# Selective-scan layers on one core: two scan tiles per step instead of one, and one activation table set for exp and ln

## The chip, the cores and the metric

The kernel runs on one core of a Trainium2 chip. The metric is device microseconds of one execution. The engines are named as in the profile: PE is TensorE's matmul (PEld its weight loads), DVE is VectorE, ACT is ScalarE, POOL is GpSimd, SP is SyncE, whose queue issues the DMAs.

## The reference

A stack of four layers acts on four images of 64 x 64 tokens with 96 channels. Every layer is a normalisation, a mixer with a residual, another normalisation and a feed-forward block in a small float format with a residual. Layer 0's mixer is a gated recurrence over the 4096 tokens with 16 states per channel. The mixers of layers 1 to 3 project to 192 channels, convolve 3 x 3, and run a selective scan in four directions; cut to what matters, it is

```python
delta = softplus(dts + bias)
def step(h, inp):
    u_l, dl, b_l, c_l = inp
    dA = jnp.exp(dl[..., None] * A)
    h = dA * h + (dl * u_l)[..., None] * b_l[:, :, None, :]
    y = jnp.einsum('bkdn,bkn->bkd', h, c_l)
    return (h, y)
_, ys = lax.scan(step, h0, (u_t, d_t, B_t, C_t))
y = ys + Dp * u
```

The four directions are added, normalised, multiplied by silu(z) and projected back to 96 channels.

## The kernel before, in words

The kernel writes the order of each engine's instructions out by hand: a wrapper (class `InOrder`, line 71) chains all instructions of one engine in the order in which the program emits them. Since this wrapper makes every instruction, all rows of the profile carry its line, L78, and are told apart by the names of their tiles.

There are three stretches. `gated` (line 1034) does layer 0 for all images: 32 strips of 512 tokens with 12 tiles each. `scans` (line 839) does layers 1 to 3, which are 12 stages (an image and a layer), and a tail does what is left of the last image.

A stage of `scans` has 24 items: two directions of time, four segments of 1024 tokens, three chunks of 128 channel rows (a row is a channel in one of two orders of the tokens). An item has 16 tiles, one for each state n, so there are 12 x 24 x 16 = 4608 tiles. For one tile [128, 1024]

- `c_rows` (line 867) reads the C row of state n from DRAM, broadcast over 64 partitions, by two DMAs into a `c` buffer (six of them);
- `decays` (line 877) makes `da` = exp(delta * A) on ACT (three buffers);
- `b_rows` (line 883) broadcasts the B row into PSUM by two matmuls of `sel` with `bs`, tile `bc`; there are two such buffers, so the B rows of one tile wait until the scan two tiles before has read its own;
- `scan` (line 892) multiplies `bc` by `du` = delta * u on DVE, in place ("product" below), and then runs the recurrence over the 1024 tokens as one TENSOR_TENSOR_SCAN into `h` (three buffers);
- `carry` (line 908) copies the last state out on ACT, `times_c` (line 914) multiplies `h` by `c` on POOL;
- `accumulate` (line 934) adds the result over the states in PSUM (`acc`, one buffer) by eight matmuls of 64 x 64 (sixteen at an item's first tile); `take` (line 945) copies the sum out on ACT, and `store` (line 949) writes it by four DMAs.

The loop at line 975 takes one tile k per step: carry k-1, C rows and decays k+2, B rows k+1, times_c k-1, product k, `beside`, scan k, accumulate k-3. `beside` (line 999) puts side work between product and scan: it pumps the chains that prepare the next item (`prepare_chunk`, line 805: matmuls, softplus, du) and the next segment (line 775), and takes a step of a job. A job (line 717) is everything else: the mixers' ends, feed-forward, input projections and convolutions of the stage before or after, cut into pieces at each `yield`; `rate` pieces of every chain run per tile.

ScalarE evaluates exp, ln, softplus, silu and sigmoid from tables, and a load is put in front of an activation whose function isn't in the set that is loaded. A norm is `measure` (line 217: mean and variance), a logarithm, and `settle` (line 232: exp(-0.5 ln v), refined on POOL). The norms queue in `pending`, and `logarithms` (line 242) does all that are queued together: behind a softplus, at n = 11 of each item, or when a job had no other work for `patience` pumps. Chains wait until their norm is `known`.

Of the kernel before, what the change touches and what calls it, by code (L numbers as in the profile page):

```python
# [13 lines left out]
F8 = mybir.dt.float8e5  # L14
# [85 lines left out]
def metaformer(ctx: ExitStack, tc: tile.TileContext, x, l0_ab, l0_rest, ssm, ffn, out):  # L100
# [31 lines left out]
    def settle():  # L132
        banks["free"] += banks["back"]
        banks["back"] = 0

    def pump(chain):

        if chain is None or chain.done:
            return False
        if callable(chain.need):  # L140
            if not chain.need():
                return False
        elif chain.need and banks["free"] < 1:
# [13 lines left out]


    ident = const("ident", [128, 128])
    make_identity(nc, ident)  # L160
# [7 lines left out]

    mod32 = sb(3, "h", [NB3, 32])
    dve.tensor_tensor(mod32, ident[0:NB3, 0:32], ident[0:NB3, 32:64], ALU.add)  # L170
# [12 lines left out]
    dve.tensor_tensor(fold, fold, ident[:, 96:128], ALU.add)  # L183
    ones = const("ones", [128, 1])
    pool.memset(ones, 1.0)
    minus = const("minus", [128, 1])
    pool.memset(minus, -1.0)
    small = {}
# [6 lines left out]
    for layer in range(4):  # L195
        raw = sb(3, "da", [128, F_N])
        sp.dma_start(out=raw, in_=ffn[layer])
        w1 = const(f"w1_{layer}", [C, HID], F8)
        dve.tensor_copy(w1, raw[0:C, 0:HID], saturate=False)
        w2 = const(f"w2_{layer}", [128, 3, C], F8)  # L200
        dve.tensor_copy(w2, raw[:, F_W2:F_B1].rearrange("p (h c) -> p h c", h=3), saturate=False)
        b8 = sb(3, "h", [128, 3 + C], F8)
        dve.tensor_copy(b8, raw[:, F_B1:F_N], saturate=False)
        b = const(f"b_{layer}", [128, 3 + C])
        dve.tensor_copy(b, b8)
        ffw.append((w1, w2, b))


    class Norm:


        def __init__(self):
            t = sb(13, "norm", [128, 3, G])
            self.v, self.r, self.nm = (t[:, i, :] for i in range(3))
            self.known = False

        def measure(self, src, width, e):
# [11 lines left out]
            act.activation(self.nm, mv[:, :, 0], AF.Copy, scale=-1.0)  # L229
            pending.append(self)  # L230

# [6 lines left out]


    pending = []  # L240

    def logarithms():
        for n in pending:
            act.activation(n.r, n.v, AF.Ln)
            n.known = True
        pending.clear()

# [322 lines left out]
    def convolve(im, layer, s, hold):  # L570
# [20 lines left out]
        for i, v in enumerate(raw):  # L591
            act.activation(v, v, AF.Silu, bias=w[:, W_CB + i : W_CB + i + 1])
        gate_z(im, s + 1, hold)
        yield
        yield
# [27 lines left out]
    def between(im, layer, dst=None):  # L623
# [32 lines left out]
        def mixers():  # L656
            for s in range(NSTRIP):
                yield lambda: done["end"] > s - 2 and (
                    layer == 0 or (done["y"] > s and hold["y", s][1].known)
                )  # L660
                if layer:
# [5 lines left out]
        def feeds():  # L667
            for s in range(NSTRIP):
                yield lambda: done["x"] > s and hold["x", s][1].known
                yield from feed_forward(im, layer, s, hold, new)  # L670
                done["end"] += 1
# [31 lines left out]
        def convolves():  # L703
            yield lambda: done["in"] > 0
            gate_z(im, 0, hold)
            yield
            yield
# [9 lines left out]
    class Job:  # L717


        def __init__(self, rounds, rate=1.4, patience=17):  # L720
            self.rounds, self.rate, self.credit = rounds, rate, 0.0
            self.patience, self.waited = patience, 0
            self.chains, self.done = [], False

        def step(self):
            self.credit = min(self.credit + self.rate, 3.0)
            while self.credit >= 1 and not self.done:
                self.credit -= 1
                while not self.done and all(c.done for c in self.chains):
                    if pending:  # L730
                        break
# [4 lines left out]
                if any([pump(c) for c in self.chains]) or not pending:  # L736
                    self.waited = 0
                    continue
                self.waited += 1
                if self.waited >= self.patience:  # L740
                    logarithms()
                    self.waited = 0

        def finish(self, eager=False):

            while not self.done:
                self.step()
                if eager and pending:
                    logarithms()
                settle()  # L750
# [54 lines left out]
    def prepare_chunk(item):  # L805
# [16 lines left out]
        act.activation(delta, delta, AF.Softplus)  # L822
        logarithms()
        yield
# [14 lines left out]
    def scans(stages, jobs, pac):  # L839
# [51 lines left out]

        def scan(k, beside):
            i, n = tiles[k]
            da, b = live.pop((k, "da")), live.pop((k, "b"))
            dve.tensor_tensor(b, i.du, b, ALU.mult)
            beside()
            h = live[k, "h"] = sb(3, "h", [128, T])
            step = slice(None, None, -1 if i.d else 1)
# [15 lines left out]
        def times_c(k):  # L914
            i, n = tiles[k]
            c = live[k, "c"]
            pool.tensor_tensor(c, live.pop((k, "h")), c, ALU.mult)

# [41 lines left out]
        start(items[0])  # L960
        c_rows(0)
        c_rows(1)
        decays(0)
        decays(1)
        b_rows(0)
        working = []
# [7 lines left out]

        for k in range(last + 5):
            q, n = divmod(k, NS)
            if k <= last:
                item = items[q]
                nxt = at(q + 1)
                if n == 0:  # L980
                    if q % per == 0:
# [4 lines left out]
                    chain = Chain(prepare_chunk(nxt), True) if nxt is not None else None  # L986
                if item.chunk == 1 and n == 4 and at(q + 2) is not None:
                    if q % per == per - 2:
# [4 lines left out]
                    segment = Chain(next_segment(items[q + 2 : q + 5]))  # L993
                if n == 8 and nxt is not None:
                    start(nxt)
                if n == 8 and nxt is not None and nxt.d == 1:
                    nxt.yf = sb(2, "y", [128, T])
                    sp.dma_start(out=nxt.yf, in_=nxt.im.y[nxt.chunk, :, nxt.seg * T : (nxt.seg + 1) * T])
            def beside():
# [8 lines left out]
            full = items[(k - 4) // NS] if k >= 4 and (k - 4) % NS == NS - 1 else None  # L1008
            if full is not None:
                take(full)  # L1010
            if 0 <= k - 1 <= last:
                carry(k - 1)
            if k + 2 <= last:
                c_rows(k + 2)
                decays(k + 2)
            if n == 11:
                logarithms()
            if k + 1 <= last:
                b_rows(k + 1)
            if 0 <= k - 1 <= last:  # L1020
                times_c(k - 1)
            if k <= last:
                scan(k, beside)
            if full is not None:
                store(full)
            if 0 <= k - 3 <= last:
                accumulate(k - 3)
            settle()
        while working:
# [4 lines left out]
    def gated(images, job, pac):  # L1034
# [6 lines left out]
        rest = sb(1, "e", [128, T])  # L1041
        sp.dma_start(out=rest[0:C, 0:L0_BIAS], in_=l0_rest[0:C, 0:L0_BIAS])
# [22 lines left out]
        def prepare(st):  # L1065
# [3 lines left out]
            yield  # L1069
            logarithms()  # L1070
            yield
            yield from norm.settle()
# [6 lines left out]
            pool.tensor_scalar(var, var, 1e-3, None, ALU.add)  # L1079
            pending.append(again)  # L1080
            yield
            logarithms()
            yield
            act.activation(again.r, again.r, AF.Exp, scale=-0.5)
# [21 lines left out]
            yield  # L1106
            act.activation(st.gate, ps[0:C], AF.Sigmoid, bias=col(at)[0:C])
            release()
            pair = [sb(2, t, [128, T]) for t in ("delta", "du", "y")]
# [68 lines left out]
        def recur(t):  # L1178
# [5 lines left out]
            dve.scalar_tensor_tensor(db, db, col(LT + i), st.du[g], ALU.add, ALU.mult)  # L1184
            h = t["h"] = sb(3, "h", [128, T])[:, 0:MM]
            dve.tensor_tensor_scan(
# [86 lines left out]
    with tc.tile_pool(name="pbig", bufs=2, space=bass.MemoryType.PSUM) as wides_pool:  # L1273
        wides.append(wides_pool)
        with tc.tile_pool(name="pl0", bufs=1, space=bass.MemoryType.PSUM) as pl0:
            gated(images, Job(between(images[0], 0), 2.6, patience=1), pl0)
        stages = [(im, layer) for layer in range(1, 4) for im in images]
# [12 lines left out]
    with tc.tile_pool(name="pend", bufs=6, space=bass.MemoryType.PSUM) as pend:  # L1290
        banks.update(free=6, back=0, pool=pend)
        Job(between(images[-1], 3, images[-1].dst), 3, patience=1).finish(eager=True)

# [115 lines left out]
```

## Time and profile before

| | us |
|---|---|
| median of 3 runs | 19251.46 (19226.88 to 19251.56) |
| the profiled execution | 19244.18 |
| its span, first to last instruction | 19242.4 |
| mean granted TensorE clock | 0.800 |

A row of groups in the profile has line, engine, operation, out<-in, shapes, count; then busy us and the mean duration of one in ns; then the engine's idle time just before these instructions and what ended most of it. A row in order of time has start and length in us, the engine, the operation, and in brackets an idle time of the engine before it. Two rows of one engine can overlap, where the next instruction starts before the end of the one before it.

The granted clock in tenths over the span, in 40 slices, and the matmul engine's busy tenths:

```profile
PE   8998787787787788788888788788888788788887
...
PEclk9998796786787797797797797797787787788775
```

The table loads are a group of their own:

```profile
L78 ACT ACT_TABLE_LOAD x1287 | 1651.2, 1283 | 37.7 <-DVE mv L78 19.8
```

### The profile page before, as it was taken

The numbers are of one execution on the slowest core, as the hardware profiler recorded it, in microseconds if no ns is written. First come the engines' busy times: TensorE is split into PE (matmuls) and PEld (weight loads), VectorE is DVE, ScalarE is ACT, GpSimd is POOL, SyncE is SP. The second block draws the span as 40 slices with busy tenths as digits, with TensorE's granted clock in tenths as the row PEclk, the third lists the DMA queues.
The fourth block names the chain that finished last, engine by engine and source line by source line (L and its number), as shares of the span: only waits on it lengthen the run. The fifth ranks groups of instructions, "written<-read, shape, count | busy, mean of one in ns | idle before, by whom it ended". The sixth has DMA issues, their size and how long they took to land.

```text
span 19242.4 us, 219783 instructions
## 1 busy us (share of the span) xinstructions
PE 15910.7 (83%) x69248; PEld 4675.9 (24%) x69248; DVE 17682.6 (92%) x13768; ACT 11062.2 (57%) x17831; POOL 13533.8 (70%) x9222
## 2 busy tenths in 40 slices
PE   8998787787787788788888788788888788788887
PEld 3332121121122222222222222222222222222323
DVE  6757999999999999999999999999999999999985
ACT  4544564555555665665665665665665665666664
POOL 3434777777777777777777777777777777777775
PEclk9998796786787797797797797797787787788775
DMA  2213666666676667667667677667676676676664
GB/s 52 51 45 93 167 189 170 167 187 171 167 194 176 171 186 185 172 186 183 171 187 182 174 191 182 170 187 187 168 192 180 171 192 179 170 198 176 168 180 115
DMA packets 1269846, 3192.04 MB, mean 166 GB/s; under 512 B 440336, under 2 KB 440560, under 8 KB 1262544
## 3 DMA queue, kind: packets, MB, share of 16 engines
q1 hardware_dynamic: 1268688, 3177.97, 62.7%
q8 instruction: 559, 9.16, 0.2%
q14 instruction: 599, 4.91, 0.1%
HBM read 2818.51 MB, written 308.28 MB: 162 GB/s over the span
## 4 chain that ended last, share of the span: by engine, by line
DVE 62%; PE 17%; ACT 10%; issue 4%; DMA 3%; POOL 3%; SPq 1%; DVEq 1%; POOLq 0%; ACTq 0%
DVE h L78 43%; DVE bc L78 16%; ACT da L78 5%; PE bc L78 4%; PE acc L78 4%; PE conv L78 2%; ACT L78 2%; DMA c<-cs 2%; POOL c L78 1%; PE dt_proj L78 1%; SPq L78 1%; DVE st L78 1%; PE y_t L78 1%; PE c L78 1%; POOL du L78 1%
## 5 line engine op out<-in xcount | busy, mean ns | idle before, releaser
L78 POOL TENSOR_TENSOR c<-h,c 128x1024 f32<-128x1024 f32 (+1 forms) x4992 | 11337.3, 2274 | 5052.2 <-DVE h L78 3027.9
L78 DVE TENSOR_TENSOR_SCAN h<-da,carry,bc 128x1024 f32<-128x1024 f32 x4608 | 10798.8, 2343 | 559.6 <-POOL c L78 53.5
L78 PE MATMUL acc<-c,twice 64*64 64x512 f32 x36864 | 6386.0, 770 | 35.5 <-POOL c L78 31.2
L78 ACT ACTIVATE da<-delta,decay 128x1024 f32<-128x1024 f32 x4608 | 5285.0, 1148 | 1687.0 <-DVE h L78 1680.0
L78 PE MATMUL bc<-bs,sel 96*128 96x512 bf16 x9216 | 3509.2, 470 | 2769.7 <-DVE h L78 2671.1
L78 DVE TENSOR_TENSOR bc<-du,bc 128x1024 f32<-128x1024 f32 x4608 | 5567.0, 1208 | 181.5 <-PE bc L78 170.8
L78 ACT COPY carry<-h 128x1 f32<-128x1 f32 x3456 | 652.8, 189 | 3929.1 <-DVE h L78 3924.3
L78 PEld LDWEIGHTS <-sel 96*128 96x128 bf16 x9216 | 563.8, 102 | 7896.7 <-DVE h L78 6245.7
L78 PEld LDWEIGHTS acc<-c,twice 64*64 64x64 f32 x36864 | 1149.8, 156 | 2898.8 <-issue 2020.8
L78 ACT ACT_TABLE_LOAD x1287 | 1651.2, 1283 | 37.7 <-DVE mv L78 19.8
L78 PE MATMUL conv<-pad,tap_lo 128*128 128x512 f32 x1728 | 918.7, 638 | 0.0
L78 PE MATMUL dt_proj<-rows,w 12*128 12x512 f32 x1152 | 841.3, 817 | 6.4 <-ACT delta L78 3.9
L78 ACT COPY y<-acc 128x1024 f32<-128x1024 f32 x288 | 291.6, 1012 | 808.6 <-PE acc L78 785.8
L78 PE MATMUL x_proj<-u,xp 128*108 128x512 f32 x1152 | 715.0, 739 | 20.2 <-DMA xp<-in_ssm 8.5
L78 POOL TENSOR_TENSOR du<-delta,u 128x1024 f32<-128x1024 f32 x288 | 678.9, 2357 | 1.5 <-issue 1.5
L78 ACT ACTIVATE c<-c,l_bias 128x512 f32<-128x512 f32 x384 | 263.4, 686 | 658.4 <-PE c L78 655.7
L78 PE MATMUL conv<-pad,tap_hi 128*128 128x512 f32 (+1 forms) x1152 | 606.8, 630 | 1.6 <-ACT u L78 1.6
L78 DVE TENSOR_TENSOR_SCAN h<-da,l_carry,bc 128x512 f32<-128x512 f32 x384 | 491.5, 1280 | 42.4 <-DVE bc L78 1.8
L78 PE MATMUL y_t<-ident,pad 128*128 128x128 f32 (+1 forms) x1536 | 389.2, 340 | 51.3 <-DMA pad<-y 40.6
L78 PE MATMUL bc<-rows,u 96*128 96x512 f32 x768 | 395.4, 640 | 41.6 <-DVE h L78 41.6
L78 PEld LDWEIGHTS conv<-pad,tap_lo 128*128 128x128 f32 x1728 | 339.7, 204 | 324.4 <-issue 255.1
L78 PE MATMUL bc<-xp,u 96*128 96x512 f32 x768 | 391.0, 634 | 24.2 <-DVE h L78 24.0
(143 smaller groups left out, 12353.1 us busy)
## 6 DMA issues: line engine op xcount, KB each, us to landing
c<-cs SPq DMA_DIRECT2D x9216, 256.0 KB, 4.2
u<-u SPq DMA_DIRECT2D x288, 512.0 KB, 6.7
y<-y SPq DMA_DIRECT2D x1152, 128.0 KB, 3.5
y<-y SPq DMA_DIRECT2D x144, 512.0 KB, 6.2
xr<-x SPq DMA_DIRECT2D x224, 192.0 KB, 5.0
u<-u SPq DMA_DIRECT2D x288, 128.0 KB, 3.9
pad<-y SPq DMA_DIRECT2D x288, 128.0 KB, 4.8
z<-zl SPq DMA_DIRECT2D x96, 256.0 KB, 4.5
```

The source lines that it names most:

```text
L78: ins = f(*a, **k).ins
```

## The change

The loop over tiles takes two tiles a and b = a + 1 per step. Product and scan are separate functions, and a step emits: decays b; carry a-2 and b-2; decays a+2; times_c b-2; for a-4 and then b-4: accumulate and the C rows of the tile six later; product a; `beside`; product b; scan a; `beside`; B rows a+2; times_c a; scan b; B rows b+2; and in the second step of an item `take` and `store` of the item before. There are four `h` buffers instead of three. The queue of norms, `known` and `patience` are gone: each norm's logarithm is emitted with its measuring, and `exp_and_ln` loads a table set that holds both exp and ln behind every softplus, sigmoid and group of silus. Layer 0's small weights share a buffer with its last block of weights. The diff, cut to its core:

```diff
+    def exp_and_ln():
+
+        act.preload_act_table_set("natural_log_exp_and_others")
...
             act.activation(self.v, mv[:, :, 1], AF.Identity, bias=small[e])
             act.activation(self.nm, mv[:, :, 0], AF.Copy, scale=-1.0)
-            pending.append(self)
+            act.activation(self.r, self.v, AF.Ln)
...
-                yield lambda: done["x"] > s and hold["x", s][1].known
+                yield lambda: done["x"] > s
...
         act.activation(delta, delta, AF.Softplus)
-        logarithms()
+        exp_and_ln()
...
-        def scan(k, beside):
+        def times_b(k):
+            i, n = tiles[k]
+            b = live[k, "b"]
+            dve.tensor_tensor(b, i.du, b, ALU.mult)
+
+        def scan(k):
             i, n = tiles[k]
             da, b = live.pop((k, "da")), live.pop((k, "b"))
-            dve.tensor_tensor(b, i.du, b, ALU.mult)
-            beside()
-            h = live[k, "h"] = sb(3, "h", [128, T])
+            h = live[k, "h"] = sb(4, "h", [128, T])
...
+            if on:
+                decays(b)
+            for k in (a - 2, b - 2):
+                if 0 <= k <= last:
+                    carry(k)
+            if a + 2 <= last:
+                decays(a + 2)
+            if 0 <= b - 2 <= last:
+                times_c(b - 2)
+                del live[a - 2, "h"], live[b - 2, "h"]
+            for k in (a - 4, b - 4):
+                if 0 <= k <= last:
+                    accumulate(k)
+                if k + 6 <= last:
+                    c_rows(k + 6)
+            if on:
+                times_b(a)
+            beside(2 * m)
+            if on:
+                times_b(b)
+                scan(a)
+            beside(2 * m + 1)
+            if a + 2 <= last:
+                b_rows(a + 2)
+            if on:
+                times_c(a)
+                scan(b)
+            if b + 2 <= last:
+                b_rows(b + 2)
+            if m == 1 and q >= 1:
+                take(items[q - 1])
+                store(items[q - 1])
...
             act.activation(st.gate, ps[0:C], AF.Sigmoid, bias=col(at)[0:C])
+            exp_and_ln()
```

More of the change, by code (lines that the diff above doesn't have):

```diff
@@ L166, in metaformer @@
     stacked = twice[:, 0:64]
-    mod32 = sb(3, "h", [NB3, 32])
+    mod32 = sb(4, "h", [NB3, 32])
     dve.tensor_tensor(mod32, ident[0:NB3, 0:32], ident[0:NB3, 32:64], ALU.add)
@@ L183, in metaformer @@
     dve.tensor_tensor(fold, fold, ident[:, 96:128], ALU.add)
[L184 to L187, printed above, removed]
     small = {}
@@ L201, in metaformer @@
         dve.tensor_copy(w2, raw[:, F_W2:F_B1].rearrange("p (h c) -> p h c", h=3), saturate=False)
-        b8 = sb(3, "h", [128, 3 + C], F8)
+        b8 = sb(4, "h", [128, 3 + C], F8)
         dve.tensor_copy(b8, raw[:, F_B1:F_N], saturate=False)
@@ L214, in __init__ @@
             self.v, self.r, self.nm = (t[:, i, :] for i in range(3))
-            self.known = False
         def measure(self, src, width, e):
@@ L237, in settle @@
             pool.tensor_tensor(self.nm, self.nm, self.r, ALU.mult)
[L240 to L246, printed above, removed]
     def refine(r, v):
@@ L657, in mixers @@
             for s in range(NSTRIP):
-                yield lambda: done["end"] > s - 2 and (
-                    layer == 0 or (done["y"] > s and hold["y", s][1].known)
-                )
+                yield lambda: done["end"] > s - 2 and (layer == 0 or done["y"] > s)
                 if layer:
@@ L705, in convolves @@
             gate_z(im, 0, hold)
+            exp_and_ln()
             yield
@@ L717, in metaformer, with __init__ @@
     class Job:
-        def __init__(self, rounds, rate=1.4, patience=17):
+        def __init__(self, rounds, rate=1.4):
             self.rounds, self.rate, self.credit = rounds, rate, 0.0
-            self.patience, self.waited = patience, 0
             self.chains, self.done = [], False
@@ L729, in step @@
                 while not self.done and all(c.done for c in self.chains):
-                    if pending:
-                        break
                     self.chains = next(self.rounds, None)
@@ L735, in step, with finish @@
                     break
[L736 to L740, printed above, removed]
-                    logarithms()
-                    self.waited = 0
-        def finish(self, eager=False):
+                for c in self.chains:
+                    pump(c)
+        def finish(self):
             while not self.done:
                 self.step()
-                if eager and pending:
-                    logarithms()
                 settle()
@@ L822, in prepare_chunk @@
         act.activation(delta, delta, AF.Softplus)
-        logarithms()
+        exp_and_ln()
         yield
@@ L916, in times_c @@
             c = live[k, "c"]
-            pool.tensor_tensor(c, live.pop((k, "h")), c, ALU.mult)
+            pool.tensor_tensor(c, live[k, "h"], c, ALU.mult)
         def add_quarters(i, v, lhs, start, stop):
@@ L960, in scans @@
         start(items[0])
-        c_rows(0)
-        c_rows(1)
+        for k in range(2):
+            c_rows(k)
+            b_rows(k)
         decays(0)
-        decays(1)
-        b_rows(0)
         working = []
@@ L973, in work @@
                 working[0].step()
-        for k in range(last + 5):
-            q, n = divmod(k, NS)
-            if k <= last:
+        half = NS // 2
+        for j in range(len(tiles) // 2 + 2):
+            q, m = divmod(j, half)
+            a, b = 2 * j, 2 * j + 1
+            on = b <= last
+            if on:
                 item = items[q]
                 nxt = at(q + 1)
-                if n == 0:
+                if m == 0:
                     if q % per == 0:
@@ L986, in scans @@
                     chain = Chain(prepare_chunk(nxt), True) if nxt is not None else None
-                if item.chunk == 1 and n == 4 and at(q + 2) is not None:
+                if item.chunk == 1 and m == 2 and at(q + 2) is not None:
                     if q % per == per - 2:
@@ L993, in scans, with beside @@
                     segment = Chain(next_segment(items[q + 2 : q + 5]))
-                if n == 8 and nxt is not None:
+                if m == 4 and nxt is not None:
                     start(nxt)
[L996 to L999, printed above, removed]
+                    if nxt.d == 1:
+                        nxt.yf = sb(2, "y", [128, T])
+                        t = slice(nxt.seg * T, (nxt.seg + 1) * T)
+                        sp.dma_start(out=nxt.yf, in_=nxt.im.y[nxt.chunk, :, t])
+            def beside(n):
                 pump(chain)
@@ L1006, in beside @@
                 work()
[L1008 to L1028, printed above, removed]
+                settle()
+            if on:
[22 more added lines that the diff above has]
+                b_rows(a + 2)
+            if on:
+                times_c(a)
[5 more added lines that the diff above has]
+                store(items[q - 1])
         while working:
@@ L1040, in gated @@
             sp.dma_start(out=v[0:C, 0:n], in_=l0_ab[:, i * T : i * T + n])
-        rest = sb(1, "e", [128, T])
+        rest = blocks[-1][:, 3 * LT * 128 - 4 * T : T]
         sp.dma_start(out=rest[0:C, 0:L0_BIAS], in_=l0_rest[0:C, 0:L0_BIAS])
@@ L1069, in prepare @@
             yield
-            logarithms()
-            yield
             yield from norm.settle()
@@ L1079, in prepare @@
             pool.tensor_scalar(var, var, 1e-3, None, ALU.add)
-            pending.append(again)
             yield
-            logarithms()
-            yield
+            act.activation(again.r, var, AF.Ln)
             act.activation(again.r, again.r, AF.Exp, scale=-0.5)
@@ L1107, in prepare @@
             act.activation(st.gate, ps[0:C], AF.Sigmoid, bias=col(at)[0:C])
+            exp_and_ln()
             release()
@@ L1184, in recur @@
             dve.scalar_tensor_tensor(db, db, col(LT + i), st.du[g], ALU.add, ALU.mult)
-            h = t["h"] = sb(3, "h", [128, T])[:, 0:MM]
+            h = t["h"] = sb(4, "h", [128, T])[:, 0:MM]
             dve.tensor_tensor_scan(
@@ L1275, in metaformer @@
         with tc.tile_pool(name="pl0", bufs=1, space=bass.MemoryType.PSUM) as pl0:
-            gated(images, Job(between(images[0], 0), 2.6, patience=1), pl0)
+            gated(images, Job(between(images[0], 0), 2.6), pl0)
         stages = [(im, layer) for layer in range(1, 4) for im in images]
@@ L1291, in metaformer @@
         banks.update(free=6, back=0, pool=pend)
-        Job(between(images[-1], 3, images[-1].dst), 3, patience=1).finish(eager=True)
+        Job(between(images[-1], 3, images[-1].dst), 3).finish()
 def _layer0(W_in, b_in, W_out, b_out, gamma, beta):
```

## The prediction

> **What bounds the kernel now.** I read the page's busy shares first, then the groups of instructions, then VectorE in order of time, then who waits for whom, last the stretches of one stage.
>
> ```profile
> PE 15910.7 (83%) x69248; PEld 4675.9 (24%) x69248; DVE 17682.6 (92%) x13768; ACT 11062.2 (57%) x17831; POOL 13533.8 (70%) x9222
> ...
> L78 DVE TENSOR_TENSOR_SCAN h<-da,carry,bc 128x1024 f32<-128x1024 f32 x4608 | 10798.8, 2343 | 559.6 <-POOL c L78 53.5
> ...
> L78 DVE TENSOR_TENSOR bc<-du,bc 128x1024 f32<-128x1024 f32 x4608 | 5567.0, 1208 | 181.5 <-PE bc L78 170.8
> L78 PE MATMUL bc<-bs,sel 96*128 96x512 bf16 x9216 | 3509.2, 470 | 2769.7 <-DVE h L78 2671.1
> ```
>
> VectorE is busy 92%; the 4608 scans and 4608 products are 16.4 of its 17.7 ms. The scans' idle time is 559.6 us, yet its largest named releaser explains only 53.5. VectorE in order of time shows the rest:
>
> ```profile
> 9002.12 1.23 DVE L78 TENSOR_TENSOR bc<-du,bc 128x1024 f32<-128x1024 f32 x1
> 9003.48 2.35 DVE L78 TENSOR_TENSOR_SCAN h<-da,carry,bc 128x1024 f32<-128x1024 f32 x1
> ...
> 9010.60 1.21 DVE L78 TENSOR_TENSOR bc<-du,bc 128x1024 f32<-128x1024 f32 x1
> 9011.72 0.41 DVE L78 BATCH_NORM_STATS2 st<-x 128x6 f32<-128x96 f32 x2
> 9012.04 2.33 DVE L78 TENSOR_TENSOR_SCAN h<-da,carry,bc 128x1024 f32<-128x1024 f32 x1
> 9014.29 1.21 DVE L78 TENSOR_TENSOR bc<-du,bc 128x1024 f32<-128x1024 f32 x1
> ```
>
> A scan right behind its product starts 0.13 us after the product's end (9002.12 + 1.23 = 9003.35, start 9003.48). An instruction that doesn't read its forerunner starts 0.09 us before that one's end (9010.60 + 1.21 = 9011.81, start 9011.72; 9012.04 + 2.33 = 9014.37, start 9014.29). So a dependent pair costs 0.13 + 0.09 = 0.22 us. A tile then takes 1.12 + 0.22 + 2.26 = 3.60 us, and in the trace's records 3143 of 4607 scan-to-scan distances are 3.59 to 3.61. From the first scan (1775) to the last one's end (19027) VectorE is the bound; ahead of it lies the gated layer, where PE is busy 1571 of 1775 us, behind it a tail of 216 us.
>
> PE is the engine next to the bound:
>
> ```profile
> PE bc L78 <- DVE h L78: 2667.3, 2372, 3.7
> ```
> ```profile
> DVE bc L78 <- PE bc L78: 170.8, 136, 7.0
> ```
> ```profile
> 3190.00:3790.00 600.00, 465.27 (x1922) 99.18 (x1921) 578.90 (x465) 337.50 (x553) 444.14 (x262) 0.69 0.63 164
> 3790.00:4190.00 400.00, 358.60 (x1496) 100.48 (x1496) 381.79 (x223) 257.33 (x409) 297.64 (x211) 0.92 0.70 189
> 4190.00:4611.00 421.00, 342.74 (x1303) 68.29 (x1304) 399.57 (x235) 196.84 (x256) 295.32 (x132) 0.68 0.66 178
> ```
>
> The first two are waits (us, times, longest). PE waits for a scan to free a B buffer in 2372 of 4608 tiles; in the others it is late when the scan ends, yet VectorE waits for it only 136 times: a buffer freed by scan k-1 is wanted by product k+1, 3.0 us later. The last three are one stage in three stretches (span, busy PE, PEld, DVE, ACT, POOL, granted clock): mixers, convolutions, scans alone. PE is 78, 90 and 81% busy, at clocks of 0.69, 0.92 and 0.68.
>
> **The change part by part.** *The order product a, product b, scan a, scan b.* Each scan now has another instruction between it and its product, so the 0.22 goes. In the trace 3708 tiles have product and scan adjacent and 899 have side work between: 3708 x 0.218 = 808 us. [...] I take the rows: both kinds stand side by side. Bounds 0 and 808.
>
> *What the order does to PE.* Its queue per step becomes accumulate a-4 and b-4, both pieces of side work, B rows a+2 (waits for scan a), B rows b+2 (waits for scan b). The last are wanted by product b+2, one product (1.12 us) after scan b ends, and take 0.06 + 0.60 to start and run at full clock. Behind that wait stand the next step's accumulations and side work; product b+2, scan a+2 and ScalarE's copies out of PSUM wait for them. So PE may be late by 0.4 us where it had 3.0, and its work for two tiles must fit into 2 x 3.38 + 0.4 = 7.2 us. From the matmul records, PE works 2.41 us beside B rows and 0.76 on them per tile: 6.34 per pair on average, with a standard deviation of 1.76 and 27% of the pairs over 7.2. What lies over sums to 851 us at the clocks granted then; with the slow shares of each pair scaled to full clock (B rows 0.60 against 1.03 us), 209 us.
>
> Between these the clock decides. [...] In this trace, of 1674 windows of 3.4 us at half clock with PE over 95% busy, 60% were followed by full clock. So 60% of the way from 851 to 209: 466 us. To it come PE's waits for ACT, POOL and VectorE inside side work, 307 us in the scans, now under cover; in the share of pairs that is late (about 30%) they show: +90. I take 560; ends 209 and 851 + 307 = 1158.
>
> *ACT.* exp(da) of b opens a step and is wanted 4.5 us into it; ahead of it in the queue stands the last step's side work. Per pair ACT has 2 x 1.15 + 2 x 0.19 plus about 1.9 of the rest, of 6.8: covered; without cover each us of softplus burst (load, 1.06, load) would fall on scan b. *Table loads:* 1287 become about 857, counted in the code as two per softplus (288 chunks), strip's Silu (96), first gate (12) and sigmoid (32). In the scans that is ACT's idle time: 0 (VectorE waits 8.3 us for da in all). In the gated layer 185 become about 85: 100 x 1.3 = 130 us on ACT beside a PE-bound loop, but at strip boundaries the norms hold ScalarE's queue up and PE behind it; bounds 0 and 130, I take 50. In the tail the loads are 5.3% of the chain of 216 us: 11 us.
>
> *Moved, at nothing.* C rows of a+2 in SP's queue wait for accumulate a-4, about 1.8 us into the step, and land 4.2 us later; POOL wants them at 6.8 + 4.5 = 11.3, so 5 us cover it, and other DMAs behind them on SP wait no longer than PE is late. POOL: product c of b first, side work, product c of a; 2 x 2.36 + about 0.9 side per 6.8 us. Copying y out of acc follows ACT's side work and is wanted a step later. The fourth h buffer takes the 54 us of waits on POOL's c away at most. Side jobs no longer wait for batched logarithms: the same work, earlier in the stage. Bounds for these together: -54 and +100; I take 0.
>
> Sum against the profiled execution, 19244.2 (span 19242.4 and 1.8 around it): 19244 - 808 + 560 - 50 - 11 = 18935. The median of the runs is 7 above it: **18940**.
>
> **The rivals.** *PE keeps up:* busier, it gets full clock and only 209 us come back: 19251 - 808 + 209 - 61 = 18590. For it: 0.92 where it is 90% busy. Against: mixers and scans alone, 0.68 at 80%. *PE becomes the bound, slower:* one lost buffer's slack at B rows b+2. It decides once more than 808 + 61 = 869 us come back, 0.38 us per pair. At today's clocks with every wait uncovered, 1158: 19540. For it: 851 is already close. Against: full windows do raise the clock. [...]
>
> **How the numbers follow.** My forecast, part of the gap kept (18700 to 19200): 0.54. PE keeps up: 0.20. Within 0.2% (39 us, about what a measurement of this kernel can tell from no change): 0.08. PE the bound: 0.14. Gap stays: 0.04. So faster 0.74, same 0.08, slower 0.18. The range, 18480 to 19400, takes in the first two with their bounds and the slower side up to a payback of about 1000 us.
>
> **What would show it.** VectorE in order of time: product b 1.12 behind product a, scan a 1.12 behind product b, scan b 2.26 behind scan a, and a pair at 6.77 where PE is not late. VectorE's waits for PE's bc at 500 to 600 us instead of 171, on the first product of a step; the granted clock in the scans over today's 0.79. Table loads near 857; the gated layer shorter by some 50 us. I am wrong if scans still start 0.13 behind, if that wait stays under 250 or passes 900, or if VectorE waits for da or c.

## The result and the profile after

The changed kernel is slower: 19542.67 us (median of 4 runs, 19528.11 to 19585.04) against 19251.51 us for the kernel before on the same chip, a ratio of 1.0156 (95% interval 1.0143 to 1.0169). The forecast was 18940 us with a range up to 19400. The profiled execution took 19547.1 us, with a span of 19545.3 us and a mean granted clock of 0.823.

The busy line of the changed kernel, and the three groups that were shown of the kernel before:

```profile
PE 15456.9 (79%) x69248; PEld 4899.9 (25%) x69248; DVE 17420.3 (89%) x13768; ACT 10485.1 (54%) x17401; POOL 13484.3 (69%) x9220
```
```profile
L78 DVE TENSOR_TENSOR_SCAN h<-da,carry,bc 128x1024 f32<-128x1024 f32 x4608 | 10595.3, 2333 | 80.9 <-ACT da L78 39.4 <-POOL c L78 20.8 <-ACT carry L78 14.3
L78 DVE TENSOR_TENSOR bc<-du,bc 128x1024 f32<-128x1024 f32 x4608 | 5488.4, 1217 | 1120.7 <-PE bc L78 1106.2 <-PE dt_proj L78 7.4
...
L78 PE MATMUL bc<-bs,sel 96*128 96x512 bf16 x9216 | 3212.1, 447 | 3206.8 <-DVE h L78 3096.6 <-DMA c<-cs 87.6 <-DMA y<-y 5.5
```

The idle time has changed places. Ahead of the scans it fell from 559.6 to 80.9 us: the gap between a product and its own scan is gone. Ahead of the products it rose from 181.5 to 1120.7 us, and nearly all of that is put down to PE's `bc`, the B rows. VectorE in order of time and who waits for whom:

```profile
8999.69 1.23 DVE L78 TENSOR_TENSOR bc<-du,bc 128x1024 f32<-128x1024 f32 x1
9000.83 4.58 DVE L78 TENSOR_TENSOR_SCAN h<-da,carry,bc 128x1024 f32<-128x1024 f32 x2
9005.33 2.33 DVE L78 TENSOR_TENSOR bc<-du,bc 128x1024 f32<-128x1024 f32 x2
9007.57 4.58 DVE L78 TENSOR_TENSOR_SCAN h<-da,carry,bc 128x1024 f32<-128x1024 f32 x2
```
```profile
DVE bc L78 <- PE bc L78: 1106.2, 609, 15.1
```
```profile
PE bc L78 <- DVE h L78: 3139.4, 2302, 10.1
PE x_proj L78 <- DMA u<-u: 187.1, 89, 5.2
```

Two products and two scans now take 9007.57 - 9000.83 = 6.74 us where nothing is late. VectorE waits for B rows 609 times instead of 136, and in the records all 609 waits stand ahead of product a, the first of a step; none stands ahead of product b. PE still waits 3139 us for scans to give B buffers back: it is idle more and late more in the same run. The wait of `x_proj` for `u` was 5.3 us before. The same stage in three stretches (mixers, convolutions, scans alone; columns as before):

```profile
3231.00:3831.00 600.00, 421.36 (x1872) 106.23 (x1864) 550.48 (x452) 312.93 (x536) 426.56 (x261) 0.74 0.64 160
3831.00:4231.00 400.00, 344.14 (x1437) 103.66 (x1438) 364.84 (x217) 251.95 (x394) 289.46 (x202) 0.89 0.70 179
4231.00:4679.00 448.00, 331.37 (x1404) 82.64 (x1406) 420.91 (x252) 209.83 (x279) 314.95 (x141) 0.78 0.72 182
```

The clock did rise in the first and third stretch (0.69 to 0.74, 0.68 to 0.78), in the second it fell (0.92 to 0.89), and PE is busy less in all three. The bill by stretches of the span: the gated layer 1775.4 to 1800.1 (+25), the scans 17251.5 to 17536.7 (+285), the tail 215.5 to 208.5 (-7).

Where PE is late can be read from its instructions in order of time. PE's rows of the changed kernel, then VectorE's in the same stretch:

```profile
7451.19 1.03 PE L78 MATMUL bc<-bs,sel 96*128 96x512 bf16 x2 [1.63 <-DVE h L78]
7452.15 3.69 PE L78 MATMUL acc<-c,twice 64*64 64x512 f32 x16
7455.77 2.07 PE L78 MATMUL dt_proj<-rows,w 12*128 12x512 f32 x2
7457.77 1.89 PE L78 MATMUL bc<-bs,sel 96*128 96x512 bf16 x4
```
```profile
7453.40 4.58 DVE L78 TENSOR_TENSOR_SCAN h<-da,carry,bc 128x1024 f32<-128x1024 f32 x2
7458.84 2.36 DVE L78 TENSOR_TENSOR bc<-du,bc 128x1024 f32<-128x1024 f32 x2 [0.87 <-PE bc L78]
```

PE first stands still for 1.63 us, waiting for a scan. Then both accumulations and the side work come in one block of 5.6 us, and the B rows of both next tiles (x4) lie behind it. Tile a's buffer was free since scan a ended, about 7455.7, two us before its B rows began. They are late not because their buffer is late but because of what stands ahead of them in the queue.

Over all 609 waits, the records give the stretch from the end of one step's B rows b to the start of the late B rows a+2 that follow as 7.2 us on average. PE is busy for 6.4 us of it, where about 5.4 would fit (worked out under "Why the prediction was wrong"). PE's idle time in these stretches, counted up to the length of the wait behind each, sums to 431 of the 1106 us. By this count at most two fifths of the wait come from waits inside the side work, and the rest is work that does not fit at the clock granted (0.82 on average in the scans).

### The profile page after: what moved, and what is told of

The parts are those of the page before. It is cut to its first block, busy times and chain, and to the rows that moved or that the text cites. A ratio compares the mean times of both kernels' runs of the same rounds, so it can differ in the third digit from the quotient of the medians.

```text
span 19545.3 us, 224167 instructions
## 1 busy us (share of the span) xinstructions
PE 15456.9 (79%) x69248; PEld 4899.9 (25%) x69248; DVE 17420.3 (89%) x13768; ACT 10485.1 (54%) x17401; POOL 13484.3 (69%) x9220
## 5 line engine op out<-in xcount | busy, mean ns | idle before, releaser
L78 DVE TENSOR_TENSOR_SCAN h<-da,carry,bc 128x1024 f32<-128x1024 f32 x4608 | 10595.3, 2333 | 80.9 <-ACT da L78 39.4
L78 DVE TENSOR_TENSOR bc<-du,bc 128x1024 f32<-128x1024 f32 x4608 | 5488.4, 1217 | 1120.7 <-PE bc L78 1106.2
L78 PE MATMUL acc<-c,twice 64*64 64x512 f32 x36864 | 6088.5, 789 | 52.7 <-POOL c L78 43.8
L78 PE MATMUL bc<-bs,sel 96*128 96x512 bf16 x9216 | 3212.1, 447 | 3206.8 <-DVE h L78 3096.6
L78 PEld LDWEIGHTS acc<-c,twice 64*64 64x64 f32 x36864 | 1529.6, 171 | 3493.4 <-issue 2634.9
L78 PEld LDWEIGHTS <-sel 96*128 96x128 bf16 x9216 | 674.6, 103 | 5768.6 <-DVE h L78 4969.9
L78 ACT ACTIVATE delta<-dt_proj,w 128x512 f32<-128x512 f32 x576 | 394.9, 686 | 1491.9 <-PE dt_proj L78 1491.3
L78 ACT COPY carry<-h 128x1 f32<-128x1 f32 x3456 | 567.2, 184 | 1063.9 <-DVE h L78 1059.0
L78 PE MATMUL dt_proj<-rows,w 12*128 12x512 f32 x1152 | 753.2, 737 | 1.5 <-DVE rows L78 1.3
L78 POOL CAST hq<-ff_h 128x512 fp8e5<-128x512 f16 x384 | 234.0, 610 | 266.9 <-ACT ff_h L78 256.2
```

The costliest lines, as they stand in the source:

```text
L78: ins = f(*a, **k).ins
```

## The experiments

Theory 1 at first: the order on VectorE took the slack from B rows b+2. Theory 2: the norms and tables cost. Rival 3: C rows, waiting in SP's queue for accumulations, hold up side DMAs behind them. Times are medians; ratios are to the kernel before in the same batch, with 95% intervals.

**1. The norms and tables alone** (the loop of before, three `h` buffers, with the change's table set and immediate logarithms).

```diff
-            pending.append(self)
+            act.activation(self.r, self.v, AF.Ln)
...
-        logarithms()
+        exp_and_ln()
```

> The loop of before (one tile per step, three h buffers), with the change's table set and its logarithms at once. Theory 1 (the loss is B rows that have lost their slack): the tables are worth little either way, 19150 to 19290, with about 857 table loads and VectorE's wait for PE's bc near the 171 us of before. Theory 2 (the loss comes from the norms: side work no longer held back is denser and ScalarE's order is worse): 19450 or more. Rival 3 (C rows in SP's queue): as theory 1.

Measured: 19336.79 us, ratio 1.0043 (1.0027 to 1.0059). Table loads fell to 857 as counted, and 550 us of loading with them, yet the kernel is slower: gated layer +39, scans +42, tail -9 us by the spans. That lies between what the two theories expected (up to 19290; 19450 or more). VectorE's waits for da came to only 8.3 us in the kernel before, so taking work off ScalarE had nothing to give in the scans; why the kernel lost 84 us was not found.

**2. The order alone** (the change's loop, with the norms as before).

```diff
...
+            if m == 5:
+                logarithms()
             beside(2 * m + 1)
...
```

> Two tiles per step and four h buffers, with the norms' queue and patience of before. Theory 1: as slow as the changed kernel, 19450 to 19650, scans 0.09 us ahead of their forerunner's end, VectorE waiting about 1000 us for PE's bc. Theory 2: 19250 or faster, since the order closes the 0.22 us gap and the norms are as before. Rival 3: as theory 1.

Measured: 19596.19 us, ratio 1.0177 (1.0161 to 1.0192); wait for B rows 1175 us, as theory 1 expected. The loss comes with the loop; in it the change's norms were worth 54 us (19596 against 19543).

**3. The product written to SBUF**, into the `h` buffer, with the scan in place on it, so that a product frees its B buffer.

```diff
-            dve.tensor_tensor(b, i.du, b, ALU.mult)
+            h = live[k, "h"] = sb(4, "h", [128, T])
+            dve.tensor_tensor(h, i.du, live.pop((k, "b")), ALU.mult)
...
-                b[:, step],
+                h[:, step],
```

> The changed kernel, but the product is written into the h buffer in SBUF and the scan runs in place on it, so that a B buffer in PSUM is free when its product has ended, not its scan: B rows b+2 have over 4 us of slack instead of 0.4. Theory 1: VectorE's wait for bc falls from 1106 to 200 us or less and the time to 18450 to 18750. Theory 2: 19400 to 19550. Rival 3 (PE stands still for late u loads, 187 us): PE's lateness of up to 5 us is partly covered, 18700 to 19000. If a product into SBUF takes longer than 1.21 us, each 0.1 us adds 460 us.

Measured: 24351.89 us, ratio 1.2645 (1.2626 to 1.2664). The wait for B rows did fall, but the scan itself became slower. Its groups of VectorE, and below them POOL's product with c:

```profile
L78 DVE TENSOR_TENSOR_SCAN h<-da,carry,h 128x1024 f32<-128x1024 f32 x4608 | 16201.2, 3547 | 50.1 <-ACT da L78 47.7
L78 DVE TENSOR_TENSOR h<-du,bc 128x1024 f32<-128x1024 f32 x4608 | 5388.0, 1199 | 465.9 <-PE bc L78 360.1 <-POOL c L78 69.5 <-ACT carry L78 9.3
```
```profile
L78 POOL TENSOR_TENSOR c<-h,c 128x1024 f32<-128x1024 f32 (+1 forms) x4992 | 15129.0, 3048 | 3914.2 <-DVE h L78 1477.6 <-ACT c L78 505.9 <-PE acc L78 395.6
```

A scan takes 3547 ns instead of 2333, and POOL's product 3048 instead of 2275. In the records, 63 scans during which POOL rested took 2341 ns on average, so writing in place is not what slows them. Of all 4608, 1302 took under 2.45 us and 1934 took 4.2 us or more; every one of the long ones began while an instruction was running on POOL, against 28% of the short ones. In the changed kernel, where one input is in PSUM, no scan took over 2.35 us: the 2658 that began while POOL ran took 2337 ns on average, the 1950 others 2328. So the scan, now with both inputs in SBUF, is slow where POOL is at work, and POOL's products, which got longer too, fit being held up by the scan. As a test of theory 1 the run is worthless: 4608 x 1.21 = 5580 us of longer scans cover all else. It does show why the product stays in PSUM: 2333 ns a scan against 3547.

**4. C rows behind the side work** in SP's queue.

```diff
             for k in (a - 4, b - 4):
                 if 0 <= k <= last:
                     accumulate(k)
-                if k + 6 <= last:
-                    c_rows(k + 6)
...
             beside(2 * m + 1)
+            for k in (a - 4, b - 4):
+                if k + 6 <= last:
+                    c_rows(k + 6)
```

> The changed kernel, with the four C row DMAs of a step emitted behind both pieces of side work, so that side DMAs (u above all) no longer stand behind a wait for accumulate in SP's queue. Rival 3: PE's 187 us of waits for u nearly vanish and VectorE's for bc lose some 300 us: 19200 to 19300. Theory 1: only the late starts of segments are helped, 19400 to 19500. Theory 2: no change, 19540.

Measured: 19353.98 us, ratio 1.0048 (1.003 to 1.0066): 189 us back, between what rival 3 (up to 19300) and theory 1 (19400 or more) expected. PE's wait of `x_proj` for `u` falls from 187 to 3 us, VectorE's for `xr` from 85 to 23 us, and its wait for B rows from 1106 to 937. So rival 3 is a real part of the loss: 189 of the 291 us between the medians of the two kernels. How it looks in the changed kernel, SP's queue first, then PE:

```profile
6009.90 2.38 SPq L78 DMA_DIRECT2D y<-y  x4
6016.21 2.40 SPq L78 DMA_DIRECT2D c<-cs  x4
6018.65 1.53 SPq L78 DMA_DIRECT2D u<-u  x3
```
```profile
6025.95 3.75 PE L78 MATMUL x_proj<-u,xp 128*108 128x512 f32 x4 [5.17 <-DMA u<-u]
```

SP stands from 6012.3 to 6016.2 at C rows that wait for an accumulation; the loads of `u` queue behind them, `x_proj` waits 5.17 us for them, and VectorE's next product, at 6030.6, then waits 5.61 us for the B rows behind `x_proj`.

**5 and 6. Half of the accumulation's matmuls left out**, in the changed kernel and, as a control, in the kernel before (an item's last tile keeps all, and so does the extra pass at its first tile).

```diff
-            for k in range(2):
+            for k in range(2 if start or stop else 1):
```

> The changed kernel with half of the accumulation matmuls of each tile left out (all but an item's first and last tile), so that PE has about 0.7 us less to do per tile; the sums it stores are therefore not the reference's. Theory 1 (PE, without slack before B rows b+2, is what VectorE waits for): the wait of VectorE for B rows falls from 1106 us to under 350 and the time to 18550 to 18900. Rival (the time went to things that are not PE's load: side DMAs held up in SP's queue behind C rows, the tables, the order of ScalarE): B rows stay late, over 800 us, and the time stays above 19300.

> The control: the kernel before with the same half of the accumulation matmuls left out (the sums are not the reference's). Theory 1: VectorE is the bound there, PE is not, so the time moves by no more than its waits for B rows: 19080 to 19260. If PE's load limited the kernel before as well, it falls below 19000.

Measured: 19585.22 us (ratio 1.0175, 1.016 to 1.019) and 19247.36 us (1.0003, 0.9994 to 1.0013): nothing. Read by itself the first would refute theory 1, but PE was not lightened. The group in the changed kernel, whole and without half of its matmuls:

```profile
L78 PE MATMUL acc<-c,twice 64*64 64x512 f32 x36864 | 6088.5, 789 | 52.7 <-POOL c L78 43.8 <-DMA c<-cs 8.3
L78 PE MATMUL acc<-c,twice 64*64 64x512 f32 x19584 | 6087.4, 797 | 50.3 <-POOL c L78 46.2 <-DMA c<-cs 3.8
```

With 36864 matmuls the group takes 6088.5 us, with 19584 it takes 6087.4, and one matmul lasts about as long (789 and 797 ns). Added up, the matmuls last 4.8 and 2.6 times the group's busy time: those of 64 x 64 ran beside each other, and leaving out one of two passes freed no time. The runs say nothing about PE's load.

**7. VectorE back in the one-tile order**, all else as changed.

```diff
-                times_b(b)
-                scan(a)
+                scan(a)
+                times_b(b)
```

> The changed kernel, all else kept (four h buffers, C rows, take and store, tables), with VectorE's order put back to product a, scan a, product b, scan b. Theory 1: the 0.22 us per tile come back, about +800 us, and B rows get their slack back, so that VectorE's wait for them falls from 1106 us to about 200: the two nearly cancel, 19350 to 19500. Rival (what makes PE late is the rest of the change, not the order on VectorE): the wait stays over 800 us, and the time is 20000 or more.

Measured: 20131.24 us, ratio 1.0457 (1.0441 to 1.0473); the wait for B rows is still 934.3 us, 559 times. The 0.22 us came back (in the records about 3600 scans start again 0.13 us behind their products), and the wait gave only 172 us for it. Theory 1 in its first form falls: the lost slack behind the scans was not what made PE late. The buffer of B rows a+2 was now free earlier, and yet they began when the queue let them, late in 83% of the steps (60% in the changed kernel). The theory that replaced it: B rows a+2 and b+2 both stand at the end of a step in PE's queue, behind both accumulations and both pieces of side work. Whatever VectorE's order, that block has to fit between the end of the step before's scan b and the next step's product a.

**8. That order chosen by the load** given to PE, on top of 4.

```diff
+            heavy.append(side + 0.5 * (load[0] - was))
+            if on and heavy[-1] > HEAVY:
+                scan(a)
+                times_b(b)
+            elif on:
                 times_b(b)
                 scan(a)
```

> The kernel with the C rows behind the side work, and with the order of each pair chosen when the program is written: product a, product b, scan a, scan b where the side work given to PE around it is light, product a, scan a, product b, scan b for the third of the pairs where it is heavy (over 3.0 us by a count of matmul columns). Theory 1: two thirds of the gain of the order stay (about 540 of 808 us), and the heavy pairs get back 1.3 to 2.3 us of slack, so that the wait for B rows falls from 937 us to 300 to 500: 18900 to 19200, faster than both kernels. If lateness is not tied to heavy side work, the wait stays over 700 us and the time is 19350 to 19550.

Measured: 19502.84 us, ratio 1.013 (1.0113 to 1.0147); the wait only fell from 937 to 854 us. A miss. The new theory explains it afterwards: the one-tile order's slack can't be used while both B rows are behind the block.

**9 and 10. B rows a+2 ahead of the second piece of side work**, in the changed kernel and in that of 7.

```diff
-            beside(2 * m + 1)
             if a + 2 <= last:
                 b_rows(a + 2)
+            beside(2 * m + 1)
```

> The changed kernel with one move: B rows a+2 are given to PE ahead of the second piece of side work instead of behind it; B rows b+2 stay at the end of the step. Theory 1 in a new form (what was lost is not the slack behind the scans, it is PE's queue: both B rows of a step lie behind both accumulations and both pieces of side work, so that this block has to fit between scan b and product a+2, 5.4 us, whatever VectorE's order is): product a+2 then waits for the first piece only, and the block may last until product b+2, 0.55 us longer. VectorE's wait for B rows falls from 1106 us to 650 to 850, the time to 19200 to 19400. Old theory 1 (only the slack of B rows b+2 counts): the wait stays at 1000 us or more, the time within 60 us of 19543.

> The same move, with VectorE's order put back to product a, scan a, product b, scan b. New theory 1: now each B rows has both its own place in PE's queue and 3.6 us of slack, as in the kernel before, and VectorE's wait for them falls from 934 us to 250 to 450: 19450 to 19700, 450 us or more under the 20131 of that order without the move. If the lateness has another cause (DMAs or ScalarE), it stays over 19950.

Measured: 19271.77 us (ratio 1.0005, 0.9993 to 1.0016) and 19548.54 us (1.0154, 1.0139 to 1.0169). One line moved gives 271 and 583 us back. VectorE's wait, in the changed order and in the one-tile order:

```profile
DVE bc L78 <- PE bc L78: 716.9, 563, 14.7
```
```profile
DVE bc L78 <- PE bc L78: 285.5, 237, 12.1
```

Both are inside what the new theory expected, and outside what the old one did. In the changed order the records put 263 us of the wait ahead of product a, where 1106 stood, and 454 ahead of product b, where there was none: the move takes from one and gives to the other.

**11 and 12. A step further**: the accumulation of b-4 also behind B rows a+2, with the C rows late; and the same with the order by load.

```diff
-            for k in (a - 4, b - 4):
-                if 0 <= k <= last:
-                    accumulate(k)
+            if 0 <= a - 4 <= last:
+                accumulate(a - 4)
...
             if a + 2 <= last:
                 b_rows(a + 2)
+            if 0 <= b - 4 <= last:
+                accumulate(b - 4)
             beside(2 * m + 1)
```

> The changed order of VectorE, with three moves together: C rows behind the side work, B rows a+2 ahead of the second piece, and the accumulation of tile b-4 behind B rows a+2. New theory 1 with the queue of SP: 190 us from the C rows and 200 to 350 from the queue of PE: 18950 to 19200, faster than both kernels; VectorE's wait for B rows 500 to 700 us. If the two gains are one and the same: 19250 to 19350.

> The same three moves, with VectorE's order of a pair chosen by the side work given to PE (the one-tile order for the third of the pairs that is heavy). New theory 1: now the slack of the one-tile order can be used, since B rows b+2 lie right behind the second piece; VectorE's wait for B rows falls to 250 to 450 us and the gap costs 270 us: 18850 to 19150, below the kernel with the three moves alone or equal to it. Otherwise 270 us above it less what the wait falls by.

Measured: 20236.03 us (ratio 1.0509, 1.0492 to 1.0527) and 19761.9 us (1.0265, 1.025 to 1.0281). Both missed by far, and the first is the slowest of this kind. PE's rows of the first:

```profile
9022.54 0.60 PE L78 MATMUL bc<-bs,sel 96*128 96x512 bf16 x2 [0.77 <-DVE h L78]
9023.07 1.09 PE L78 MATMUL acc<-c,twice 64*64 64x512 f32 x8
9024.09 1.13 PE L78 MATMUL conv<-pad,tap_lo 128*128 128x512 f32 x2
9025.06 0.60 PE L78 MATMUL bc<-bs,sel 96*128 96x512 bf16 x2
```
```profile
DVE bc L78 <- PE bc L78: 1722.7, 1279, 5.6
```

B rows a+2 can't start before scan a ends, and B rows b+2 are wanted 2.26 + 1.12 us later. What stands between has 2.26 + 1.12 - 0.6 - 0.66 = 2.1 us. The accumulation takes 1.02 us of that in these rows (9023.07 to 9024.09) and about 1.85 at half clock (3.69 us for two at 7452.15 in the changed kernel, granted 0.50), and a piece of side work like the convolution's above needs another 1.0. Now B rows b+2 begin late in 70% of the steps. The block had been too long on one side; I made it too long on the other. Run 14 below differs from the first of these in the place of that accumulation alone, and takes 19091.52 us: the misplaced accumulation costs 1145 us.

**13. Every odd tile's accumulation left out** of the changed kernel (but an item's last): the test of PE's load that 5 should have been.

```diff
-            add_quarters(i, h, stacked, False, n == NS - 1)
+            if n % 2 == 0 or n == NS - 1:
+                add_quarters(i, h, stacked, False, n == NS - 1)
```

> The changed kernel with the accumulation of every odd tile left out (but for an item's last), 1.4 us of PE per pair by the matmul records; the sums are not the reference's. If PE's load in the block before B rows a+2 is what VectorE waits for: the wait falls from 1106 us to 350 to 550, the time to 18800 to 19050. If waits inside the block (on DMAs, ScalarE, POOL) make it late rather than load: the wait stays over 850 us, the time above 19300.

Measured: 19411.75 us, ratio 1.0081 (1.0066 to 1.0097), the wait 979 us. By both of its marks (over 850 us, above 19300 us) this is the rival's side: waits inside the block, not load. But PE's load did not fall as was meant. One stage (9014 to 10463 us) of the changed kernel, then of this one, with span, busy PE, PEld, DVE, ACT, POOL, granted clock:

```profile
9014.00:10463.00 1449.00, 1140.36 (x5428) 351.24 (x5424) 1351.59 (x994) 811.29 (x1302) 1061.08 (x659) 0.83 0.71 178
```
```profile
9014.00:10463.00 1449.00, 1095.60 (x4096) 321.68 (x4096) 1363.49 (x1001) 816.85 (x1311) 1064.13 (x661) 0.72 0.72 180
```

A quarter of the matmuls is gone, and PE is busy only 4% less: the granted clock fell from 0.83 to 0.72, and the matmuls that were left took longer (one of the B rows' 505 ns on average, against 447). In the whole span 2016 accumulations of 1.32 us, 2660 us, are left out, and PE's busy time fell by 702. Most of what was taken off PE came back as slower matmuls. So this run doesn't settle how much of the wait is load and how much is waits inside the block; the count by records above (at most 431 of 1106 us in waits) is the nearest there is. 9, 10 and 11 do show that the place in the queue alone moves the wait by hundreds of us either way.

**14 to 16. Both repairs together** (4 and 9), with the change's norms; with the norms as before; and with the one-tile order for the sixth of the pairs with a heavy piece.

```diff
+            if a + 2 <= last:
+                b_rows(a + 2)
             beside(2 * m + 1)
+            for k in (a - 4, b - 4):
+                if k + 6 <= last:
+                    c_rows(k + 6)
```

> The changed kernel with both repairs: C rows behind both pieces of side work in SP's queue, and B rows a+2 ahead of the second piece in PE's queue. If they add up: 19543 - 190 - 270 = 19080, and with what they share (the x_proj wait on u had already fallen to 67 us by the move of the B rows alone) 19080 to 19200, faster than both kernels. If C rows come too late for POOL there, 19270 or more.

> The same two repairs on the order alone: the table set and the norms' logarithms as in the kernel before. The old order lost 84 us by the new norms; the new order, unrepaired, gained 54 by them. If the new norms cost by denser side work in PE's queue, this is 50 to 100 us under e15; if their gain in the new order was real, 30 to 60 us above it.

> Both repairs, and VectorE in the one-tile order for the sixth of the pairs in which a piece of side work gives PE over 2.2 us by a count of matmul columns. If the wait left is that of heavy pieces: the gap costs 0.17 x 2304 x 0.44 = 170 us and the wait falls by 250 to 400 us, so 80 to 230 us under e15. If it is spread over all pairs: up to 150 us above e15.

| kernel | us | ratio (95% interval) | wait for B rows, us |
|---|---|---|---|
| 14: both repairs | 19091.52 | 0.9914 (0.99 to 0.9927) | 610.7 |
| 15: and the norms as before | 18951.54 | 0.9848 (0.9835 to 0.9862) | 556.1 |
| 16: as 14, order by load | 19105.15 | 0.9919 (0.9906 to 0.9931) | 449.6 |

The repairs add up: the changed kernel 19543, C rows late 19354, B rows between 19272, both 19092, which is 451 us where the single ones sum to 460. In 16 the wait fell by 161 us, less than the 250 expected at least, and the time rose by 14 us, so that the gap in a sixth of the pairs cost about the 170 expected: the heavy pieces are part of the wait that is left, and this is no cheap way to be rid of it. 15 is 140 us under 14, more than the 50 to 100 expected if the new norms cost; so they cost 84 us in the loop of before, gave 54 in the changed loop, and cost 140 in the repaired one. The wait lines of 15, the fastest kernel here, 1.5% below the one before:

```profile
DVE bc L78 <- PE bc L78: 556.1, 536, 7.8
```
```profile
PE acc L78 <- ACT y L78: 40.0, 43, 2.7
```
and of 14:
```profile
PE acc L78 <- ACT y L78: 130.6, 63, 5.0
```

Between 14 and 15, whose table loads are 857 and 1281, the spans differ by 30 us in the gated layer, 113 in the scans and -6 in the tail. In the scans PE waits 91 us longer for ScalarE's copy of y out of `acc`. That fits immediate norms that get into ScalarE's queue ahead of that copy, but it was only read, not tested. Whether the table set or the immediate logarithms cost was not tried.

## Why the prediction was wrong

**The order (step 1: -808 us) held, and was worth 742.** Scan b starts 2.257 us behind scan a where nothing is late, and a scan starts 0.09 us before the end of the product ahead of it in place of 0.13 behind its own. VectorE's time in the scans, less its gaps over 0.2 us, fell from 16986 to 16244 us. About 45 us of what is missing from 808 are products b that start just behind product a's end instead of 0.09 us before it (475 of 1810 pairs that stand side by side). Run 7 shows the price coming back: 20131. No run shows a reason for the gap to stay, which the forecast gave a chance of 0.04; in the rows it closed.

**PE's payback (step 2: +560 us) is the step that failed.** It came to 1027: VectorE's gaps over 0.2 us in the scans went from 266 to 1293 us in the records, 935 of it in the wait for B rows. The mechanism, PE late with B rows, was right; two terms of it were mis-sized, and runs show where each comes from:

- *The window.* The step took B rows b+2 as the late ones and let the work of two tiles have 7.2 us. (Its marks did expect the waits on the first product of a step; its sum did not follow them.) But B rows a+2 stand behind the same block and are wanted one product earlier, and all 609 waits were for them. With nothing late, the block has from 0.66 us after a scan b, when the B rows behind it are done, until 0.66 before the product a that wants the next B rows a+2, one pair (6.74 us) after that scan's end: some 5.4 us; with both B rows that is 6.7 us, not 7.2. Over 6.7, the step's own count of the records of before sums to 1230 at granted and 373 at full clock; 60% of the way is 716, and with the 90 of the step 806. By this estimate, reading the queue one entry nearer would have moved the forecast by 250. Moving that entry gave back 271 (run 9), but the two are not the same quantity, since the move brought product b waits that it had not had.
- *Moved, at nothing.* "Other DMAs behind them on SP wait no longer than PE is late" was wrong; they delay the side work, which then delays the B rows behind it. This is the 189 us of run 4. 806 + 189 = 995, near the 1027 measured; this sum is made after the fact. With both faults mended (run 14) VectorE's gaps come to 826 us, 560 over before: the very payback forecast, though that it is so close is luck.

The step's inputs were also off, the other way. PE's busy time in the scans of before, 14177 us over 2304 pairs, is 6.15 us per pair; a count that takes in PE's waits inside side work and for DMAs gives 6.33, close to the step's 6.34. If that is what the step counted, its +90 adds these waits a second time. By busy time alone 600 to 700 us would lie over 7.2, not 851, so this made the forecast too slow, not too fast, and part of the nearness of 995 to 1027 is luck.

The clock in the scans rose as forecast (0.79 to 0.82), and run 13 shows it moving the other way. Counted again in the trace of before, 1021 windows, not 1674, were at half clock with PE over 95% busy, with the same 60% followed by full clock, against 3% of the less busy windows at half clock. Nearly all clock records of that trace last 3.41 us or a multiple of it. Whether 60% of the way was the right share between 851 and 209, no run tests.

**Table loads.** The count was right (857), the worth wrong in sign: the gated layer was to get 50 us shorter and got 25 longer (39 in run 1), and in the scans the norms cost 42 alone. The tail gained 7 of 11. **Sum:** 25 + 285 - 7 = 303 us, the difference of the spans, and in the scans -742 + 1027 = 285.

**The rivals.** "PE becomes the bound, slower", 19540 with a chance of 0.14, is what happened in size. Its mechanism was half right: PE late at B rows, but at a+2 and by its queue, not at b+2 by the one lost buffer's slack (run 7). The mark "I am wrong if that wait passes 900" was passed at 1106.

## What to carry to other kernels

When two steps of an in-order loop are fused into one, list every engine's queue for the fused step and ask of each entry what now stands ahead of it, not only when its inputs are free. Here VectorE's gain was real, but more than all of it was lost to waits again, 451 us through two entries alone (B rows behind side work on PE, C rows ahead of side DMAs on SP); two moved lines turned +1.6% into -0.9%, and leaving the norms alone made it -1.5%. Every move has two sides: putting one entry too many behind the same point (run 11) cost more than the fault had.

## What the runs showed of the hardware that I had not expected

- Work taken off PE came back as a slower clock: 25% fewer matmuls in a stage, 4% less busy time, granted clock 0.83 to 0.72, one matmul of the B rows 505 ns instead of 447 (run 13).
- f32 matmuls of 64 x 64 ran beside each other: 36864 or 19584 of them took 6088.5 and 6087.4 us (run 5).
- A scan on VectorE with both inputs in SBUF took 2.3 us or up to 4.45, those of 4.2 or more always begun while POOL was at work (run 3); with one input in PSUM it took 2.33, and none over 2.35 (the changed kernel).
